# Layer 3 of a four-layer graph network: gathered rows in other places, the table's rows in the last weight matrix

## Chip, core and metric

The kernel runs on one core of one Trainium2 chip. Its time is the device time of one execution in microseconds, and less is better. The profile is one execution on that core, taken by the hardware profiler.

## What is computed

Four layers follow each other on x (2708 nodes x 512 features) with a weighted adjacency matrix adj (2708 x 2708). Each has the form x = x + f(relu(layernorm(x)), adj). Layer 0 is a weighted aggregation, layer 1 an attention, layer 2 two aggregations with dense layers between. The change is in layer 3:

```python
def _L3_gnn_ref(input_features, adj, W, b):
    ...
    A = (adj != 0).astype(input_features.dtype)
    hidden = input_features @ W + b
    deg = jnp.sum(A, axis=0)
    return A @ hidden / deg[:, None]
...
# layer 2: what comes just before
h = jax.nn.relu(adj @ (x @ W1) + b1)
h = jax.nn.relu(adj @ (h @ W3) + b3)
return jnp.tanh(h @ Wf + bf)
```

## The kernel before

**Tiles.** The 2708 nodes make NT = 22 row tiles of 128 (the last, tile 21, has 20 rows). The adjacency is sparse towards the later nodes. So a row tile takes the first DENSE = 6 column tiles whole, and of the other columns only those in which one of its rows has a nonzero. Of these a list was made in layer 0, in chunks of 128 columns: CHUNKS gives 0, 10, 9, 8 chunks for row tiles 0 to 3, seven each for 4 to 7, six for most that follow, and two for tile 21.

**Layer 2** goes through the row tiles in `order_2` (0, then from 6 on, and 1 to 5 last). For each, `aggregated` sums the dense part (right-hand sides ghi, glo and gs of `g_parts`, one set for each of the six dense tiles) and the listed part. For the latter `gather` (L935) lets POOL fetch 128 rows of a table in DRAM for each chunk with an indirect DMA, into one of NGG = 8 tiles gg0 to gg7, in turn. Then come two projections, `project3` (L900): with wf, the last weight matrix but one, whose three parts lie in wa0 to wa2 of the pool wset; after tanh, residual and norm, with w, the last one, whose three parts lie in wb0 to wb2 of wsetb. The result is one row tile of `hid`, the table of layer 3, written to DRAM (L1294), and for tiles from 6 on to `hidr` as well.

**Layer 3** needs A @ hid, with A of zeros and ones. Products are single-pass: `split_h` splits each right-hand side into a rounded high part (ScalarE, L1111) and a remainder (VectorE, L1113), and `add_h` (L1171) makes one matmul of each. There are three kinds of work:

- `whole_h(m)`: the six dense tiles (ghi, glo) with masks a_hi from the stored marks `nz` (L1184).
- `listed_products(m)`: the gathered rows of row tile m. The high part takes one of six tiles of `part_room` (v_hi, v_lo, v_s, two buffers each), the remainder stays where the row was gathered. For the first row tile `behind` (L164) holds the part tiles until dense tile 4 has been split.
- `full_steps()`: row tiles 0 to 3 (FULL) have no usable list and take the whole table, so `load_full` brings rows 768 to 2707 of hid into SBUF: four tiles of 128 rows in each of four buffers (16 loads on SP's queue, L1222). Their high parts go to gs1 to gs5, in turn. The 16 steps are interleaved with the other row tiles, from the third on; the first four take dense tiles alone.

**Places for gathered rows.** `gather_h(m)` takes one place for each chunk from the generator `room()`. Before the change that is: the four quarters of wr (the raw weights' buffer); then again and again eight gg tiles and the four quarters of wb0, wb1 or wb2. Thus row tile 4 has wr (4) and gg (3), row tile 5 gg (5) and wb0 (2), row tile 6 wb0 (2) and gg (5), and row tile 7 gg (3) and wb1 (4). A place can be written only when its former contents have been read.

**Order.** Row tiles 4 to 20 (21 in the middle) are taken in `order_3`. The gathers of the first two are put into the program at the last row tile of layer 2, before its last two projections, the third's right after; from then on gathers are AHEAD = 3 row tiles in front. The program's order gives priorities only: each engine's own order is drawn up by the compiler, which brings an instruction forward when its buffers and inputs are there. Within an engine's queue, the order is then fixed, and POOL's gathers wait in it for their places.

`split_w` and `project3` are those of layer 2; they are unchanged. The functions that the change touches:

Of the kernel before, what the change touches and what calls it, by code (L numbers as in the profile page):

```python
# [9 lines left out]
FP = mybir.dt.float32  # L10
# [12 lines left out]
P = 128  # L23
# [13 lines left out]
DENSE = 6  # L37
# [5 lines left out]
def kernel(  # L43
# [29 lines left out]
    N, D = x.shape  # L73
    H, _, DK = wk_d.shape
# [3 lines left out]
    NCD = D // P  # L78
# [8 lines left out]
    def rows(t):  # L87
        return min(P, N - t * P)
# [63 lines left out]
    def span(t):  # L152
        return slice(t * P, t * P + rows(t))
# [8 lines left out]
    def behind(dst, last):  # L162

        nc.vector.tensor_copy(dst, last)  # L164

    def load_w(pool, src, name, first=None):
        w = pool.tile([P, NCD, D], FP, name=name)
        if first:
            first(w)
        nc.sync.dma_start(out=w, in_=src.rearrange("(c p) k -> p c k", p=P))  # L170
        return w
# [45 lines left out]
    wset = short.enter_context(tc.tile_pool(name="wset", bufs=1))  # L217
# [6 lines left out]
    with tc.tile_pool(name="l0_slab", bufs=2) as slabs, tc.tile_pool(  # L224
        name="l0_h", bufs=1
    ) as hp, tc.tile_pool(name="l0_w", bufs=2) as wp, tc.tile_pool(
        name="l0_acc", bufs=2, space=PSUM
    ) as ps_acc, tc.tile_pool(name="l0_small", bufs=1, space=PSUM) as ps_small, tc.tile_pool(
        name="l0_list", bufs=3, space=PSUM
    ) as ps_list, tc.tile_pool(name="l0_tr", bufs=1, space=PSUM) as ps_tr, tc.tile_pool(  # L230
        name="l0_y", bufs=1, space=PSUM
# [181 lines left out]
        NGG = NT - DENSE  # L413
# [352 lines left out]
        for m in range(NT):  # L766
# [45 lines left out]
            if m == NT // 2 + 6:  # L812
                wr = load_w(wset, w1_d, "wr", lambda w: behind(w[:1, 0, :1], xt[:1, :1]))
                w1 = split_w(wset, wr, "wa")
                wr = load_w(wset, w3_d, "wr")
# [12 lines left out]
    gp = short.enter_context(tc.tile_pool(name="g", bufs=1))  # L828
    wsetb = short.enter_context(tc.tile_pool(name="wsetb", bufs=1))
# [8 lines left out]
    NGG = 8  # L838
# [15 lines left out]
    def gathered():  # L854
        name = f"gg{gather_slot[0] % NGG}"
        gather_slot[0] += 1
        return gp.tile([P, D], FP, name=name)
# [217 lines left out]
    wr = load_w(wset, wf_d, "wr")  # L1075

    for m in order_m:
        n = rows(m)
        parts = aggregated(m, first_parts, first_product, g1d, bias1, marked=True)
        if m == 0:  # L1080
            wf = split_w(wset, wr, "wa")
            wr = load_w(wset, w_d, "wr")
# [43 lines left out]
    def room():  # L1126


        quad = wset.tile([P, NCD, D], FP, name="wr")
        for c in range(NCD):  # L1130
            yield quad[:, c, :]
        i = 0
        while True:
            for _ in range(NGG):
                yield gathered()
            quad = wsetb.tile([P, NCD, D], FP, name=f"wb{i % 3}")
            i += 1
            for c in range(NCD):
                yield quad[:, c, :]

    places_h, part_slot = room(), [0]

    def part_room():
# [73 lines left out]

    def load_full():
        for i, t0 in enumerate(range(DENSE, NT, NCD)):
            quad = wset.tile([P, NCD, D], FP, name=("wa0", "wa1", "wa2", "wr")[i])  # L1220
            for t in range(t0, min(t0 + NCD, NT)):
                nc.sync.dma_start(out=quad[: rows(t), t - t0, :], in_=hid[span(t)])  # L1222
                full_h[t] = quad[:, t - t0, :]
# [89 lines left out]
    for i, m in enumerate(order_3):  # L1313
        listed_products(m)
        if i < AHEAD:
            whole_h(m, DENSE - 1)
        finish_h(m)
        if i == 0:
            load_full()
        if i + AHEAD < len(order_3):  # L1320
            k = order_3[i + AHEAD]
            gather_h(k)
            whole_h(k)
        if i > 1:
            next(steps, None)
        if i == 1:
            some = wp.tile([P, 1], FP, name="some", bufs=1)
            nc.vector.tensor_reduce(some, bad, AX.X, ALU.add)
            tot = ps_t.tile([P, 1], FP, name="pt")
            nc.tensor.matmul(tot, ones, some, start=True, stop=True)  # L1330
            nc.vector.tensor_scalar_min(some, tot, 1.0)
            nc.vector.tensor_copy(flag, some)
# [8 lines left out]
    with tc.If(general > 0):  # L1341

        with tc.tile_pool(name="l0_g", bufs=2) as gp, tc.tile_pool(
            name="l0_gh", bufs=1
# [53 lines left out]
        with tc.tile_pool(name="l1_qkv", bufs=1) as qkvp:  # L1398
# [6 lines left out]
            with tc.tile_pool(name="l1_pw", bufs=1) as pwp, tc.tile_pool(  # L1405
                name="l1_ph", bufs=2
            ) as php, tc.tile_pool(name="l1_px", bufs=3) as pxp, tc.tile_pool(
                name="l1_pps", bufs=2, space=PSUM
# [43 lines left out]
            with tc.tile_pool(name="l1_bias", bufs=2) as bp, tc.tile_pool(  # L1452
                name="l1_p", bufs=2
            ) as pp, tc.tile_pool(name="l1_pT", bufs=3) as ptp, tc.tile_pool(
                name="l1_x", bufs=1
            ) as xp, tc.tile_pool(name="l1_st", bufs=4) as stp, tc.tile_pool(
                name="l1_s", bufs=2, space=PSUM
            ) as ps_s, tc.tile_pool(name="l1_t", bufs=2, space=PSUM) as ps_t, tc.tile_pool(
                name="l1_o", bufs=1, space=PSUM
# [84 lines left out]
        with ExitStack() as gen:  # L1544
# [8 lines left out]
            gp = l2.enter_context(tc.tile_pool(name="g", bufs=2))  # L1553
# [213 lines left out]
```

## Time and profile before

Three runs took 1498.87, 1499.95 and 1506.9 us.

| What | Value |
|---|---|
| median of the runs | 1499.95 us |
| the profiled execution's own time | 1489.76 us |
| its span, first to last instruction | 1488.0 us |
| mean granted TensorE clock | 0.941 |
| TensorE busy | 1298.3 us (87%) |
| VectorE busy | 946.2 us (64%) |
| ScalarE busy | 690.3 us (46%) |
| POOL busy | 657.6 us (44%) |
| moved by DMA | 349.04 MB, mean 235 GB/s |
| the 65 gathers of hidr into gg | 68.5 us busy, 1053 ns each |

Busy time is the time in which an engine worked on at least one instruction, and idle time stands with the event that ended it, its releaser. "Issue" there is idle time for which the profile shows no releaser, "remote" a releaser that it couldn't name. Layer 3 begins at about 1290 us of the span and ends with it. In instruction names, L987 is line 987 of the kernel, and "gg<-hidr,idx_h" an instruction that writes a tile gg and reads hidr and idx_h; numbers of buffers are left out, so wb stands for wb0 to wb2. PE is TensorE, PEld its weight loads, DVE VectorE, ACT ScalarE, SP the queue from which most plain transfers are issued.

### The profile page before, as it was taken

Reading aid. Unit: us, or ns where it says so; the run is one execution under the profiler, and the core shown is the slowest. Engines: PE = TensorE matmul, PEld = TensorE weight load, DVE = VectorE, ACT = ScalarE, POOL = GpSimd, SP = SyncE. Lnnn points to the kernel's source line nnn. Section 1 sums busy time; section 2 is a strip of 40 time slices with the busy share of each in tenths; the row PEclk is TensorE's granted clock in tenths of the full one; section 3 lists DMA queues with packets and bytes.
Section 4 is the critical chain, followed back from the end, with each engine's and each line's share of the span. In section 5 each row is a group of like instructions: output and inputs, shape, how many; then the busy total and the mean of one; then the engine's idle time right before and its main releaser. Section 6 shows DMA issues by size and latency. Waiting matters only on the chain.

```text
span 1488.0 us, 15510 instructions
## 1 busy us (share of the span) xinstructions
PE 1298.3 (87%) x4430; PEld 774.4 (52%) x4430; DVE 946.2 (64%) x1932; ACT 690.3 (46%) x1051; POOL 657.6 (44%) x673
## 2 busy tenths in 40 slices
PE   3987687878958849988999999899999999877997
PEld 1333233333423337745665666466666666555776
DVE  3685776869969769743343446365666656665686
ACT  5965543463256246432333334344445444554453
POOL 1254366565754432054544442244334335326652
PEclk9997789899989979999999999999999999988999
DMA  9977887978797498366777777756555666557885
GB/s 349 375 244 249 268 272 242 315 242 247 250 341 284 145 308 279 131 220 209 252 222 233 237 233 234 243 176 187 174 173 170 195 195 202 175 193 221 275 261 159
DMA packets 200056, 349.04 MB, mean 235 GB/s; under 512 B 26406, under 2 KB 113024, under 8 KB 196229
## 3 DMA queue, kind: packets, MB, share of 16 engines
q1 hardware_dynamic: 149177, 200.80, 40.7%
q0 software_dynamic: 46032, 145.05, 31.2%
q10 hardware_dynamic: 4752, 2.10, 0.6%
q8 instruction: 37, 0.61, 0.2%
q14 instruction: 58, 0.48, 0.1%
HBM read 284.58 MB, written 63.29 MB: 234 GB/s over the span
## 4 chain that ended last, share of the span: by engine, by line
PE 51%; issue 5%; DMA 3%; DVE 2%; another core or an unknown queue 2%; POOL 1%; ACT 1%; SPq 0%; DVEq 0%; ACTq 0%; POOLq 0%
PE aggs L987 14%; PE main L900 9%; PE agg L984 8%; PE mixed L900 4%; PE aggs L984 4%; PE pt L875 3%; PE agg L1171 2%; PE aggs L1171 2%; DMA raw<-in_adj_t_dram 1%; PE aggs L999 1%; PE agg L900 1%; PE pt L1171 1%; POOL wb L935 1%; PE mixed L1171 1%
## 5 line engine op out<-in xcount | busy, mean ns | idle before, releaser
L987 PE MATMUL aggs<-gg,ac 128*128 128x512 f32 (+1 forms) x520 | 232.3, 594 | 3.4 <-DMA gg<-g1d,idx_g 3.4
L935 POOL DMA_INDIRECT gg<-g2d,idx_g x130 | 131.1, 1008 | 220.2 <-PE aggs L987 170.7
L935 POOL DMA_INDIRECT gg<-g1d,idx_g x130 | 133.9, 1030 | 180.1 <-PE aggs L987 109.0
L778 PE MATMUL acc<-h,inc 128*128 128x512 f32 (+1 forms) x348 | 171.1, 632 | 19.6 <-DVE inc L630 14.1
L562 POOL DMA_INDIRECT ac<-in_adj_t_dram,idx_a x130 | 127.9, 984 | 133.4 <-DMA lst<-ac 62.3
L987 PEld LDWEIGHTS aggs<-gg,ac 128*128 128x128 f32 (+1 forms) x520 | 97.9, 189 | 110.6 <-issue 103.0
L580 POOL DMA_INDIRECT h<-h0d,idx_g x111 | 117.2, 1056 | 57.0 <-issue 28.7
L971 ACT ACTIVATE a_hi<-raw 128x384 fp32r<-128x384 f32 x84 | 43.6, 520 | 167.3 <-issue 92.2
L778 PEld LDWEIGHTS acc<-h,inc 128*128 128x128 f32 (+1 forms) x348 | 66.7, 201 | 99.0 <-issue 81.5
L984 PE MATMUL agg<-ghi,a_hi 128*128 128x512 f32 x252 | 114.8, 456 | 3.3 <-ACT a_hi L971 2.4
L158 PE MATMUL yacc<-wvo,hT 128*128 128x512 f32 (+1 forms) x176 | 91.0, 663 | 28.8 <-issue 23.3
L778 PE MATMUL acc<-h,incl 128*128 128x512 f32 (+1 forms) x222 | 102.3, 609 | 0.0
L984 PE MATMUL agg<-glo,a_lo 128*128 128x512 f32 x252 | 102.2, 405 | 0.0
L972 DVE TENSOR_TENSOR a_lo<-raw,a_hi 128x384 fp32r<-128x384 f32 x84 | 47.3, 563 | 85.3 <-ACT a_hi L971 51.0
L984 PE MATMUL aggs<-gs,a_s 128*128 128x512 f32 x252 | 100.3, 401 | 0.6 <-DVE gs L204 0.6
L935 POOL DMA_INDIRECT gg<-hidr,idx_h x65 | 68.5, 1053 | 51.1 <-issue 11.3
L881 DVE SCALAR_TENSOR_TENSOR v_lo<-pt,v_hi 128x512 fp32r<-128x512 f32 (+1 forms) x88 | 56.5, 664 | 41.8 <-ACT v_hi L880 23.4
L862 DVE SCALAR_TENSOR_TENSOR u<-aggs,u 128x512 f32<-128x512 f32 x42 | 28.9, 687 | 77.9 <-PE aggs L987 68.3
L158 PEld LDWEIGHTS yacc<-wvo,hT 128*128 128x128 f32 (+1 forms) x176 | 35.2, 209 | 77.4 <-issue 66.1
L778 PEld LDWEIGHTS acc<-h,incl 128*128 128x128 f32 (+1 forms) x222 | 42.9, 195 | 54.4 <-issue 53.0
L880 ACT ACTIVATE v_hi<-pt 128x512 fp32r<-128x512 f32 (+1 forms) x88 | 48.6, 578 | 45.6 <-PE pt L875 35.8
L542 DVE MAX8 top<-ar 128x8 f32<-128x2708 f32 (+1 forms) x22 | 65.4, 2971 | 0.0
(307 smaller groups left out, 2812.3 us busy)
## 6 DMA issues: line engine op xcount, KB each, us to landing
ar<-in_adj_dram SPq DMA_DIRECT2D x27, 1354.0 KB
raw<-in_adj_t_dram SPq DMA_DIRECT2D x122, 192.0 KB
slot<-x SPq DMA_DIRECT2D x41, 256.0 KB
at<-in_adj_t_dram SPq DMA_DIRECT2D x27, 384.0 KB
ranks<-rank_b SPq DMA_DIRECT2D x20, 485.0 KB
ac<-lst SPq DMA_DIRECT2D x16, 384.0 KB
h<-in_x_dram SPq DMA_DIRECT2D x21, 256.0 KB
h0d<-h POOLq DMA_DIRECT2D x21, 256.0 KB
```

Of the source, the lines that this page charges most:

```text
L158: nc.tensor.matmul(acc[:n], hT[:, c, :n], w[:, c, :], start=(c == 0), stop=(c == NCD - 1))
L542: nc.vector.max(top[:n], ar[:n])
L562: nc.gpsimd.indirect_dma_start(out=ac[:, c, :n], out_offset=None, in_=adj_units, in_offset=bass.IndirectOffsetOnAxis(ap=idx_a[:, m, c0 + c ...
L580: nc.gpsimd.indirect_dma_start(out=g, out_offset=None, in_=h0d[:, :], in_offset=bass.IndirectOffsetOnAxis(ap=idx_g[:, m, c : c + 1], axis=0),)
L778: nc.tensor.matmul(acc[:n], a, g, start=(i == 0), stop=(i == len(pairs) - 1))
L880: nc.scalar.activation(hi[d], pt[d], AF.Relu, scale=UP)
L881: nc.vector.scalar_tensor_tensor(lo[d], pt[d], 0.0, hi[d].bitcast(FP), op0=ALU.max, op1=ALU.subtract)
L900: nc.tensor.matmul(acc[:n], a[:, c, :n], b[:, c, :], start=first and c == 0, stop=last and c == NCD - 1,)
L935: nc.gpsimd.indirect_dma_start(out=gs[c], out_offset=None, in_=gd[:, :], in_offset=bass.IndirectOffsetOnAxis(ap=index[:, m, c : c + 1], ax ...
L984: nc.tensor.matmul(acc[:n], a[:k, i, :n], b[:k], start=st, stop=sp)
L987: nc.tensor.matmul(mixed[:n], a, g, start=(c == 0 and not dense_of(m)), stop=(c == len(chunks) - 1),)
L1171: nc.tensor.matmul(bank_h(m)[: rows(m)], a, b, start=(i == 1), stop=(i == total))
```

## The change

Two functions change. In `room()`, the places from the thirteenth on: after wr and eight gg come gs1 to gs5, once (the third parts of the dense right-hand sides of layer 2), and then again and again the four quarters of wa0, wa1 or wa2 (wf) and eight gg. In `load_full()` the first three buffers of the table's rows are wb0 to wb2 (w) instead of wa0 to wa2; the fourth stays wr. Row tile 5 now has its last two rows in gs1 and gs2, row tile 6 has gs3 to gs5 and wa0, row tile 7 has seven gg, and row tile 8 has gg, the four of wa1, and gg. No instruction is added or removed.

```diff
@@ room()
         quad = wset.tile([P, NCD, D], FP, name="wr")
         for c in range(NCD):
             yield quad[:, c, :]
+        for _ in range(NGG):
+            yield gathered()
+        for t in range(1, DENSE):
+            yield gp.tile([P, D], FP, name=f"gs{t}")
         i = 0
         while True:
-            for _ in range(NGG):
-                yield gathered()
-            quad = wsetb.tile([P, NCD, D], FP, name=f"wb{i % 3}")
+            quad = wset.tile([P, NCD, D], FP, name=f"wa{i % 3}")
             i += 1
             for c in range(NCD):
                 yield quad[:, c, :]
+            for _ in range(NGG):
+                yield gathered()
@@ load_full()
         for i, t0 in enumerate(range(DENSE, NT, NCD)):
-            quad = wset.tile([P, NCD, D], FP, name=("wa0", "wa1", "wa2", "wr")[i])
+            pool, name = ((wsetb, "wb0"), (wsetb, "wb1"), (wsetb, "wb2"), (wset, "wr"))[i]
+            quad = pool.tile([P, NCD, D], FP, name=name)
             for t in range(t0, min(t0 + NCD, NT)):
                 nc.sync.dma_start(out=quad[: rows(t), t - t0, :], in_=hid[span(t)])
                 full_h[t] = quad[:, t - t0, :]
```

## The prediction, made before the changed kernel was run

> **What bounds the kernel now.** I read the page first: TensorE is busy 87% of the span, and the chain that ended last belongs to it for 51%. The change touches layer 3 alone, so next I asked for busy times by stretch from the last rows of layer 2 on. Columns: stretch, its length, then busy us (and instructions) of PE, PEld, DVE, ACT, POOL, granted clock, DMA share, GB/s.
>
> ```profile
> 1290.00:1326.00 36.00, 24.89 (x90) 18.31 (x89) 21.03 (x45) 18.56 (x28) 1.38 (x2) 0.81 0.41 137
> 1326.00:1356.00 30.00, 19.32 (x73) 14.47 (x72) 14.86 (x29) 14.15 (x25) 18.56 (x20) 0.86 0.72 230
> ...
> 1376.00:1400.00 24.00, 22.99 (x100) 18.32 (x100) 15.01 (x29) 11.51 (x20) 16.07 (x17) 1.00 0.86 271
> ...
> 1425.00:1475.00 50.00, 49.18 (x216) 39.50 (x214) 37.63 (x73) 27.20 (x49) 25.08 (x24) 1.00 0.74 224
> ```
>
> From 1376 us TensorE is full (22.99 of 24, clock 1.00). The 66 us before that, where layer 2 hands over to layer 3, are the loose part: 44.2 us busy of 66, clock 0.81 and 0.86, and POOL, which does the gathers, all but empty for the first 36 us. The timeline of POOL says why (start, length, what, and in brackets the idle time before it with its releaser):
>
> ```profile
> 1289.27 1.34 POOL L935 DMA_INDIRECT gg<-hidr,idx_h  x1 [0.30 <-issue]
> 1325.22 0.95 POOL L935 DMA_INDIRECT wb<-hidr,idx_h  x1 [34.62 <-issue]
> ```
>
> Twelve gathers (places 1 to 12: wr and gg) are out by 1290.6. The thirteenth goes to wb, which is the last weight matrix, and that is read by the last row of layer 2 until 1326.5: POOL stands 34.6 us. The timeline of TensorE then shows the holes that follow:
>
> ```profile
> 1315.90 0.79 PE L1171 MATMUL agg<-ghi,a_hi 128*128 128x512 f32 x1 [6.73 <-ACT ghi L1111]
> ...
> 1337.91 0.50 PE L1171 MATMUL aggs<-v_s,ac 128*128 128x512 f32 x1 [1.57 <-issue]
> ...
> 1343.76 0.80 PE L1171 MATMUL aggs<-gg,ac 128*128 128x512 f32 x1 [5.12 <-DVE gg L1113]
> ...
> 1355.09 0.79 PE L1171 MATMUL agg<-wb,ac 128*128 128x512 f32 x1 [3.99 <-DVE wb L1113]
> ```
>
> Three of them (10.7 us) lie in 1326 to 1356. But who ends them is not a gather. The waits of 1200 to 1488 (waiter, releaser, total us, times, longest):
>
> ```profile
> ACT v_lo L1111 <- PE aggs L1171: 16.7, 7, 5.5
> ...
> DVE slot L1211 <- remote: 7.2, 1, 7.2
> ...
> ACT v_hi L1111 <- DMA gg<-hidr,idx_h: 3.2, 4, 1.4
> ```
>
> ScalarE and VectorE, which split each gathered row in two, wait for TensorE to give back the six part tiles (v_hi, v_lo, v_s, two each), and only 3.2 us for gathered data. The 7.2 us of DVE slot (row tile 4's finish, at 1342.31) wait for products whose last matmul the trace ends at 1334.98. For row tile 5 the same step comes 5.7 us after its last matmul (1353.63 against 1347.90), for row tile 6 0.3 us (1359.99 against 1359.66). The first two fall into trains of gathers issued back to back (1325.22 to 1340.32, 1341.73 to 1351.83); before the third POOL stood 4.3 us. My reading: TensorE's releases arrive late while POOL issues gathers without a pause. That is a coincidence in one trace, not proved.
>
> **What the Trainium skill says.** "DMA: Bandwidth & Descriptors", Anatomy of one DMA — SWDGE (gpsimd) path: about 2.0 us fixed for a DMA of this queue. The trace agrees roughly: the gather issued at 1325.22 landed at 1328.16, 2.9 us. The same page, Queues, rings and completion order: a DMA engine takes turns between the queues that have work, so SP's loads and POOL's gathers slow each other; the trace shows gathers landing 6 us after issue at 1335 to 1340, behind four SP loads. "TensorE: Matmul & The Clock Gate", Part 1: after an idle window of some 3.4 us the clock is halved until TensorE is busy again. The trace agrees: half clock in 1313.55 to 1323.79, 1340.86 to 1347.69 and 1354.51 to 1357.93.
>
> **The change, part by part.**
>
> *Gathers 13 to 17 (gs1 to gs5).* Layer 2's last reader of gs is the dense part of row tile 5, whose last matmul is at 1279.88. So they go at 1290.6: five by 1.25 us (0.95 busy + 0.30), done by 1296.9. Nothing waits behind them; cost nothing, DMA is idle then (0.41).
>
> *Gathers of the wa places (18 to 21, then 30 to 33 and 42 to 45).* wa (the last weight matrix but one) has its last matmuls at 1306.2 to 1309.2. As the twelve free wb places were filled in one train (1325.2 to 1340.3, with one gg between), I expect twelve wa gathers at 1307.5 to 1322.5. Thus row tiles 4, 5 and 6 (21 rows) are in place before 1326, where now the rows of tile 6 come until 1349. Row tile 7 becomes all gg (seven places), free as tiles 4 and 5 are used, from about 1331 on.
>
> *What this is worth.* In 1326 to 1339 VectorE needs 21 x 0.6 us = 12.6 us for the splits and no long train of gathers runs beside them, so the three holes should go, and with them the half clock behind two of them: 9 matmuls from 1343.76 and 6 from 1355.09 with 0.43 instead of 0.23 us between starts, 3.0 us. Upper end 10.7 + 3.0 = 13.7 us; lower end nothing, if the part tiles come back as late as now. I take 9: next in line are row tile 7's gathers, issued from 1331.
>
> *The table's rows leave wa (L1222).* Twelve SP loads of 256 KB now run at 1307 to 1320, on idle DMA engines, and five splits (gs<-wa, wa<-wa,gs) stand in the hole. They aren't free there. The row's chain on VectorE:
>
> ```profile
> 1312.63 0.69 DVE L1286 TENSOR_TENSOR gs<-gs,u 128x512 f32<-128x512 f32 x1 [1.25 <-ACT u L1278]
> 1313.66 0.69 DVE L1113 TENSOR_TENSOR wa<-wa,gs 128x512 fp32r<-128x512 f32 x1 [0.33 <-ACT gs L1111]
> 1314.27 0.69 DVE L176 BATCH_NORM_STATS2 stats<-gs 128x6 f32<-128x512 f32 x1
> 1314.87 0.68 DVE L1113 TENSOR_TENSOR wa<-wa,gs 128x512 fp32r<-128x512 f32 x1
> 1315.46 0.18 DVE L178 BATCH_NORM_AGGREGATE mv<-stats 128x2 f32<-128x6 f32 x1
> ```
>
> Without them the statistics start at 1313.3 and end at 1314.2, and the table load and square root follow at once instead of at 1316.5 and 1317.8: 3.4 us earlier, on the path to the last product. Upper end 3.4. Lower end a loss of 3: the transposes (now 1320.48) then fall into the train of wa gathers, whose twelve could hold TensorE's release back as the 7.2 us above show. I take a gain of 1.
>
> *Where they go (wb).* wb is free from about 1324.5 to 1326.5, so SP's twelve loads (3.1 MB) and the four of wr are issued in 12 x 0.42 + 4 x 0.42 = 6.7 us there. At 372 GB/s, the most that the trace shows for such loads (1315 to 1317.5), the twelve take 8.5 us of the DMA engines, beside row tile 7's seven gathers. The table's rows themselves are late for nobody: their first matmul is at about 1380 or later. Price between 0 and 8.5; I take 1.5, since tile 7's rows are needed only after 1339. Queued behind on SP: hid of row tile 5, read only by row tile 21's gather, and the marks (nz) of tile 8, now loaded at 1353.9.
>
> *The five splits* (VectorE 5 x 0.69 = 3.4 us, ScalarE 3.1) move to after 1338, when gs1 to gs5 are free again. From 1376 VectorE is 63% busy and hides them; in the ramp it isn't hidden. Between 0 and 3.4; I take 0.5. The ring of places keeps its period of twelve, eight gg and four others, so from row tile 8 on nothing changes, and matmuls, bytes and gathers stay the same in number.
>
> **Sum.** 9 + 1 - 1.5 - 0.5 = 8 us; I add 2 (between 0 and 2) for the hole before 1315.90, which shrinks if glo no longer queues behind SP's wa loads (issued 1310.69, landed near 1315.2: 4.5 us, against 2.7 for the load issued at 1294.97). So 10 us off the profiled execution: its own time is 1489.76 (span 1488.0 and 1.8 around it), hence about 1480. The median of the runs shown is 1499.95, 10.2 higher (0.7%), for reasons the trace doesn't show; I take the gain from there: 1490.
>
> **Rivals.**
> 1. *Part tiles, not rows (no change).* For it: 16.7 against 3.2 us in the waits. If TensorE's late releases don't come from the trains of gathers, rows that are there earlier wait in SBUF. Gain: 1 to 3 us of the handover less 2 of moved work, about 1499.
> 2. *Slower: contention at 1326 to 1345.* The full 8.5 us on tile 7's rows, 3.4 us of splits and 3 us of late releases in the wa train, and no hole closed: plus 15 at worst; half of it, 1507, is what I give it. It decides once SP's loads hold tile 7's last row beyond some 1347, where TensorE would run out of tiles 4 to 6.
> 3. *All of it.* 13.7 + 3.4 + 2, less 1: 18 us, 1482.
> 4. *It doesn't do what it says:* the order of the instructions on POOL may put the wa gathers behind blocked gg places, so that only five rows come early. Then 3 to 5 us: 1496.
>
> **How the numbers follow.** My forecast (1484 to 1492) 0.44, rival 3 0.20, rivals 1 and 4 together 0.22, rival 2 0.14. A measurement of this kernel can tell about 0.5% (7.5 us) from no change: faster means under 1492.5. That gives 0.65 faster, 0.21 same, 0.14 slower. The range, 1477 to 1504, leaves out about one in ten on either side: past rival 3's value and into rival 2.
>
> **What would show it.** Right: POOL without the 34.6 us, gathers into gs at 1291 and wa at 1307 to 1322; SP's table loads at 1325 or later; the last product of wb before 1323; no TensorE hole over 2 us from 1326 to 1356 and full clock there. Wrong: holes of the same size with ACT v_lo still waiting for PE (rival 1), or ACT v_hi waiting for DMA gg in 1340 to 1355 (rival 2).

## The result, and the profile after

The changed kernel takes 1491.83 us in the median of 19 runs, against 1501.75 us for the kernel before in the runs beside it: ratio 0.9945, 95% interval [0.9923, 0.9966]. Run again on another chip it takes 1476.32 against 1490.29 us, ratio 0.9909 [0.9876, 0.9942]. The ratio leaves out two slow runs of these 19 and is not the quotient of the two medians, which is 0.9934. So it is faster by 0.5 to 0.9%, near the forecast 1490 us. Its profiled execution took 1484.00 us (span 1482.2, clock 0.945), 5.8 us less than the one before. That one is not among the 19 runs, and at 1489.76 us it lies below all of them. The line numbers of what is quoted from L1144 on are 4 or 5 higher than before, and they shift by a few lines in the experiments too.

Some words that recur: a **train** is a row of gathers that POOL issues with no more than the usual 0.30 us between them. A **hole** is idle time of TensorE. A **release** is the **rise** of TensorE's semaphore by which a matmul tells the other engines that it is done. A **burst** is a group of rises that follow each other at once.

Busy times by stretch of the changed kernel, with the same columns and stretches as above:

```profile
1290.00:1326.00 36.00, 20.81 (x76) 14.91 (x75) 16.19 (x29) 12.93 (x20) 11.75 (x12) 0.82 0.39 120
1326.00:1356.00 30.00, 27.18 (x109) 20.33 (x109) 20.90 (x48) 22.32 (x40) 15.69 (x17) 0.93 0.90 308
1376.00:1400.00 24.00, 23.38 (x100) 18.35 (x100) 17.29 (x34) 11.68 (x20) 16.50 (x17) 1.00 0.84 261
```

The second stretch is what was hoped for: TensorE 27.18 us busy instead of 19.32. The first one got worse, 20.81 instead of 24.89 (part of that is a shift: this execution is 3.0 us later when the handover begins). The forecast sum came out about right because it missed a loss and undersized a gain.

The timeline of POOL, with start, length, and the idle time before in brackets. Of each group of gathers the first and the last are shown:

```profile
1280.81 1.28 POOL L935 DMA_INDIRECT gs<-hidr,idx_h  x1 [6.58 <-PE agg L984]
...
1295.25 0.95 POOL L935 DMA_INDIRECT gg<-hidr,idx_h  x1 [0.30 <-issue]
1317.41 1.14 POOL L935 DMA_INDIRECT wa<-hidr,idx_h  x1 [21.21 <-PE main L900]
...
1331.81 0.95 POOL L935 DMA_INDIRECT wa<-hidr,idx_h  x1 [0.30 <-issue]
1339.70 1.23 POOL L935 DMA_INDIRECT gg<-hidr,idx_h  x1 [6.95 <-PE agg L1175]
```

The wait of 34.62 us is gone; one of 21.21 us stands in its place. But the gs gathers don't follow the seven gg ones: the compiler put them first, and the twelve go out from 1280.81 to 1296.20 without a pause. Twelve wa gathers follow as a second train, 10 us later than forecast. The timeline of TensorE shows what lies between:

```profile
1298.80 2.08 PE L900 MATMUL main<-wa,v_hi 128*128 128x512 f32 x4 [4.67 <-ACT go L861]
...
1325.77 0.80 PE L1175 MATMUL agg<-ghi,a_hi 128*128 128x512 f32 x1 [6.78 <-ACT ghi L1111]
...
1357.09 0.50 PE L1175 MATMUL aggs<-ghi,a_hi 128*128 128x512 f32 x1 [3.80 <-issue]
```

The first hole is new. Before, the same product (row tile 4 by wa) began without one at 1290.98. The instruction that it waits for, on ScalarE's timeline:

```profile
1298.15 0.60 ACT L861 ACTIVATE go<-main 128x512 f32<-128x512 f32 x1 [6.59 <-remote]
```

It reads a product whose last matmul ended at about 1292.9 by the trace, and its release by TensorE's semaphore is recorded at 1298.13, 1.9 us after the last gather of the train. The Trainium skill ("Perfetto Trace Analysis", Tensor Engine Instruction (MATMUL, LD_WEIGHTS)) says that a matmul's end in the profile is an estimate, and that the semaphore is raised after it, once PSUM has acknowledged the write. The order agrees with this trace; the distance of 5.2 us is what the trace shows, not the page.

In the waits of 1200 to 1488 (waiter, releaser, total us, times, longest) what answers to the former 16.7 us is:

```profile
ACT v_lo L1111 <- PE aggs L1175: 8.9, 3, 4.4
ACT v_lo L1111 <- PE agg L1175: 8.5, 4, 5.1
```

Before, the second of these stood at 0.6 us. So this wait for TensorE's releases is as long as it was (17.4 and 17.3 us; 1.4 and 5.9 us more have no named releaser). What became shorter is the time in which TensorE stands: its holes of 0.8 us and more after 1326 fell from 17.2 to 6.5 us.

Two stretches sum this up. **Handover**: from the start of row tile 2's wb product to the start of row tile 5's, the last of layer 2. **Rest**: from that product's end to the last instruction. Both are read from one execution each.

| Execution | handover | hole ahead of row tile 4's wa product | rest |
|---|---|---|---|
| before | 52.55 | none | 161.44 |
| before, again (second chip) | 52.30 | none | 162.15 |
| changed | 58.59 | 4.67 | 147.06 |
| changed, again (second chip) | 56.56 | 3.89 | 145.67 |

The change gains 14.4 and 16.5 us in the rest and gives back 6.0 and 4.3 us in the handover. The profiled times differ by less, 5.8 and 4.9 us, since the changed executions begin the handover 3.0 and 8.1 us later. Up to there TensorE's instructions come in the same order in both kernels, and in the later traces of such chips that point lies anywhere from 5.8 us ahead of the first one's to 21.2 us behind it. So single profiled times can't be compared to a few us; the medians of many runs and stretches within a trace can.

### The profile page after: what moved, and what is told of

Its sections match the earlier page's. It is cut to its first block, busy times and chain, and to the rows that moved or that the text cites. A ratio compares the mean times of both kernels' runs of the same rounds, so it can differ in the third digit from the quotient of the medians.

```text
span 1482.2 us, 15513 instructions
## 1 busy us (share of the span) xinstructions
PE 1295.9 (87%) x4430; PEld 770.6 (52%) x4430; DVE 945.8 (64%) x1932; ACT 688.4 (46%) x1051; POOL 661.2 (45%) x673
## 4 chain that ended last, share of the span: by engine, by line
PE 64%; DVE 11%; DMA 8%; issue 7%; another core or an unknown queue 4%; ACT 4%; POOL 1%; SPq 0%; ACTq 0%; DVEq 0%; POOLq 0%
PE aggs L987 14%; PE main L900 9%; PE agg L984 7%; PE acc L778 6%; PE mixed L900 5%; PE aggs L984 4%; PE agg L1175 4%; PE aggs L1175 3%; PE yacc L158 3%; PE pt L875 3%; DVE at_top L544 2%; DMA raw<-in_adj_t_dram 2%; DVE found L383 2%; PE aggs L999 1%
## 5 line engine op out<-in xcount | busy, mean ns | idle before, releaser
L562 POOL DMA_INDIRECT ac<-in_adj_t_dram,idx_a x130 | 131.4, 1011 | 120.5 <-issue 37.3
L935 POOL DMA_INDIRECT gg<-hidr,idx_h x62 | 62.9, 1015 | 49.2 <-issue 16.6
```

Of the source, the lines that this page charges most:

```text
L562: nc.gpsimd.indirect_dma_start(out=ac[:, c, :n], out_offset=None, in_=adj_units, in_offset=bass.IndirectOffsetOnAxis(ap=idx_a[:, m, c0 + c ...
L935: nc.gpsimd.indirect_dma_start(out=gs[c], out_offset=None, in_=gd[:, :], in_offset=bass.IndirectOffsetOnAxis(ap=index[:, m, c : c + 1], ax ...
```

## Experiments

The twelve runs were made on four chips, so each is compared with the kernel before on its own chip. The theories are A (gathers issued without a pause hold back TensorE's releases) and its rivals. The expectations misname some things. What they call row tile 3's wa product is row tile 4's, and "row tile 3's first wb product" is row tile 2's. The "aggregation of row tile 4" is that of row tile 5. The pauses in the kernel before cover row tiles 5 to 9, and "row tile 6 whole" is row tile 5 whole. The handover is the stretch they speak of. Edits are shown against the changed kernel where nothing else is said, and "..." marks what is left out.

### First four: one half of the change at a time, and the train turned round or paused

**e1_swap.** The places go on as before, but with wa, and the table in wb.

```diff
-        for _ in range(NGG):
-            yield gathered()
-        for t in range(1, DENSE):
-            yield gp.tile([P, D], FP, name=f"gs{t}")
         i = 0
         while True:
+            for _ in range(NGG):
+                yield gathered()
...
-            for _ in range(NGG):
-                yield gathered()
```

> The new order of weight matrices alone: rows from the thirteenth on in wa as in the change, the table in wb, but no row in gs. Theory A (a long unbroken train of gathers on GpSimd holds back TensorE's releases; the change's five gs gathers made the train at 1281 twelve long and cost some 6 us ahead of layer 3): with seven gathers in that train TensorE has no hole of 4 us ahead of the wa product of row tile 3, the train of twelve wa gathers is out by about 1325, and the ramp into layer 3 is as good as the change's; time 1484 to 1490, ratio to before 0.988 to 0.992. Theory B (only how early the rows come counts, the hole at 1294 has another cause than the train's length): five rows come later than in the change and the hole stays, so 1493 to 1499, ratio 0.994 to 0.998.

**e2_gs_only.** The five gs places stay. What follows is wb, and the table is in wa, as before.

```diff
-            quad = wset.tile([P, NCD, D], FP, name=f"wa{i % 3}")
+            quad = wsetb.tile([P, NCD, D], FP, name=f"wb{i % 3}")
...
-            pool, name = ((wsetb, "wb0"), (wsetb, "wb1"), (wsetb, "wb2"), (wset, "wr"))[i]
+            pool, name = ((wset, "wa0"), (wset, "wa1"), (wset, "wa2"), (wset, "wr"))[i]
```

> The five rows in gs alone: the rows after them in wb and the table in wa, as before. Theory A: the train at 1281 has twelve gathers, so the hole of 4 to 5 us ahead of the wa product of row tile 3 is there and the handover to layer 3 ends 6 us late; the wb gathers wait for the last wb product as before, with five fewer rows missing; time 1497 to 1504, ratio 0.997 to 1.002. Theory B: five rows early are most of what is wanted, ratio 0.993 to 0.996, as the change.

**e3_gs_last.** The changed kernel, its gs gathers held by VectorE: a copy of one element into each place waits for `last_u[0]`, the tile u of the row tile that layer 2 aggregated last.

```diff
-            yield gp.tile([P, D], FP, name=f"gs{t}")
+            late = gp.tile([P, D], FP, name=f"gs{t}")
+            behind(late[:1, :1].bitcast(FR), last_u[0][:1, :1])
+            yield late
```

> The change, with its five gs gathers put behind the aggregation of row tile 4 by one-element copies on VectorE, so that the seven gg gathers go first and the five gs ones follow them at once: the order is turned round, the train stays twelve long. Theory A: the hole stays, since TensorE's releases of 1290 to 1294 still fall into the train: 1489 to 1494, ratio 0.993 to 0.996, as the change. Rival C (it is the gs gathers going first that does it, by making the gg ones late or by waiting for row tile 4's last part tiles): the hole goes, 1484 to 1488, ratio 0.989 to 0.991.

**e4_gs_pause.** The same, but VectorE holds only the first place, POOL writes it six times over, and copies of one element on POOL hold all five places behind that:

```diff
+            if t == 1:
+                behind(late[:1, :1].bitcast(FR), last_u[0][:1, :1])
+                for _ in range(6):
+                    nc.gpsimd.memset(late, 0.0)
+                hold = gp.tile([1, 1], FP, name="hold")
+                nc.gpsimd.tensor_copy(hold, late[:1, :1])
+            nc.gpsimd.tensor_copy(late[:1, :1].bitcast(FR), hold)
```

> As the kernel with the gs gathers last, and six memsets on GpSimd between the seven gg gathers and the five gs ones, a pause of some 3 us in the train; nothing else is changed. Theory A: the releases go out in the pause, the hole of 4.7 us ahead of row tile 3's wa product is gone or under 2 us, the time 1484 to 1489, ratio 0.988 to 0.992. Theory B or C: as the kernel with gs last, or 0 to 1 us longer: the pause only delays five gathers.

| Run | ratio to before, 95% interval | handover | rest |
|---|---|---|---|
| e1_swap | 0.9968 [0.9951, 0.9985] | 53.7 | 146.3 |
| e2_gs_only | 0.9939 [0.9917, 0.9962] | 52.4 | 142.7 |
| e3_gs_last | 0.9925 [0.9899, 0.9952] | 51.0 | 143.1 |
| e4_gs_pause | 0.9955 [0.9936, 0.9973] | 55.1 | 142.7 |

Theory A fails here. All four ratios lie outside its ranges, e3_gs_last's by a hair. And e2_gs_only has the train of twelve (1216.0 to 1231.8 in its trace) and no hole ahead of row tile 4's wa product. It isn't a slow handover either, 52.4 us. But this chip is another: the kernel before takes 1418.49 us on it. And its semaphore events differ. Some 1360 of the 4430 matmuls raise TensorE's semaphore, and the trace records these rises. In each of these four runs all of them are there, 9 lie more than 0.08 us from the end of a matmul that raises it, and no two are closer than 0.08 us. In the trace of before only 1141 are recorded, 204 of them lie off such an end, and 111 follow another within 0.08 us; in that of the changed kernel 1117, 172 and 109. (Records of the other engines are missing there as well, but those that exist are on time: off are 7 of VectorE's 1279 and 2 of ScalarE's 719.) So on the first chip releases of TensorE come late and in bursts, and on this one they don't. e2_gs_only's POOL issues 61 gathers from 1261.9 to 1344.0 without a pause, and TensorE has no hole over 1.21 us in that time. Among its waits of 1200 to 1406 those for gathered data stand first:

```profile
ACT v_hi L1111 <- DMA gg<-hidr,idx_h: 13.2, 8, 5.7
...
ACT v_lo L1111 <- PE agg L1175: 6.5, 4, 3.2
...
ACT v_lo L1111 <- PE aggs L1175: 4.4, 1, 4.4
```

Over all three part tiles and the whole rest, ScalarE waits 19.7 us for data and 21.4 for TensorE there, against 5.0 and 37.7 in the trace of before (10.3 more have no named releaser). So where releases are on time more of the waiting is for rows, and five early rows bring 0.6% with no help from any train. There the rest is as short with wb (142.7) as with wa (143.1) once the five gs rows are early.

e3_gs_last isn't the test it was meant to be: the copies wait for row tile 5, so the gs gathers start 7.5 us after the last gg one and the train isn't twelve long. In e4_gs_pause the memsets push them further, into the wa gathers: 17 in one train up to 1260.0. The hole that row tile 5's handover has in every version (6.78 us at 1325.77 above) is 8.30 us there, against 6.85 in e3_gs_last.

### Second four: both kernels again, and two mixtures

**e5_after_again** and **e6_before_again** are the two kernels, unaltered.

> The changed kernel once more, unaltered, to compare the experiments with on one chip. Theory A (the gs gathers lengthen a train and cost some 6 us ahead of layer 3): the hole ahead of row tile 3's wa product is again over 4 us and the stretch from row tile 3's first wb product to the last one again some 58 us, ratio 0.993 to 0.996. Rival D (that hole belonged to one execution: the first four runs have it at 0 to 1.6 us whatever the train's length): hole 0 to 1.7 us, that stretch 51 to 54 us, ratio 0.991 to 0.994. The rest, from the last wb product to the end, 143 to 147 us under both.

> The kernel before once more, unaltered, for a trace from this chip. A and D: the stretch from row tile 3's first wb product to the last 51 to 54 us, and from there to the end 150 to 161 us, with four or more TensorE holes of over 1 us in the 90 us after the last wb product, since rows are missing. If the rest is under 147 us with no such holes, the change's gain does not come from rows that come early.

**e7_gs_last_wb** is e2_gs_only with the held gs places of e3_gs_last. **e8_gs_two** is e2_gs_only with two gs places:

```diff
-        for t in range(1, DENSE):
+        for t in range(1, 3):
```

> Five rows in gs behind the aggregation of row tile 4, the rows after them in wb and the table in wa as before: the two halves that did best, together. Rows-early theory: as the kernel with gs alone with its hole of 1.5 us ahead of the wa product gone: ratio 0.991 to 0.994. If wa and wb change nothing once five rows are early, it equals the kernel with gs last (0.9925) within 0.002; if wa's earlier rows are worth something, it is 0.002 to 0.004 above that.

> Two rows in gs in place of five, all else as in the kernel with gs alone, so that the row tile before last of the first three is whole, and the third lacks five of its seven rows until wb is free. Rows-early theory: three of five rows more to wait for at 1.25 us each leaves 3 to 4 us of the gain of 8.6 us unrealised: ratio 0.995 to 0.998. If it isn't the rows but the shift of all later gathers by five places, two fifths of the gain: ratio 0.997 to 0.999. If the gain was of the first two rows (row tile 6 whole) alone: 0.993 to 0.995.

| Run | ratio to before, 95% interval | handover | rest |
|---|---|---|---|
| e5_after_again | 0.9909 [0.9876, 0.9942] | 56.6 | 145.7 |
| e6_before_again | one run, 1489.42 us | 52.3 | 162.2 |
| e7_gs_last_wb | 0.9922 [0.9898, 0.9946] | 50.1 | 150.9 |
| e8_gs_two | 0.9939 [0.9916, 0.9962] | 51.9 | 159.0 |

On this chip (1490.29 us before) releases are late again: in the four traces 69 to 106 rises follow another within 0.08 us. The hole of the changed kernel is back in e5_after_again (TensorE's timeline), so it didn't belong to one execution, and D falls. (The ratio is better than A and D said.)

```profile
1302.49 2.08 PE L900 MATMUL main<-wa,v_hi 128*128 128x512 f32 x4 [3.89 <-ACT go L861]
```

In e7_gs_last_wb, seven gathers and the five later, it is gone, and the handover is 6.5 us shorter than in e5_after_again. It is gone in e8_gs_two as well, where two gs gathers go ahead of the seven with a pause of 0.95 us between. So going first is not what makes the hole. By time alone, though, e7_gs_last_wb can't be told from the changed kernel: their intervals overlap.

e6_before_again has three holes of over 1 us in the 90 us after the last wb product, where I had expected four or more. The rest grows with the rows that must wait for wb: 145.7 us with five gs rows and wa, 150.9 with five gs rows and wb, 159.0 with two, 162.2 with none. e8_gs_two's ratio fits the guess that the first two rows are all of the gain; its stretches don't (handover and rest together 210.9 us against 214.5 in e6_before_again, 202.3 in e5_after_again). Why its runs are that fast stays open.

### Third: pauses in the kernel before, and gs last again

**e9_before_pauses.** The kernel before, with a memset on POOL ahead of each gather of row tiles 5 to 9 (against the kernel before):

```diff
         for c in range(CHUNKS[m]):
+            if index is idx_h and m in (5, 6, 7, 8, 9):
+                nc.gpsimd.memset(gs[c], 0.0)
```

> The kernel before with nothing but a memset of 0.5 us on GpSimd ahead of each gather of the rows of row tiles 6 to 9 (its own buffer, overwritten by the gather): the gathers come 0.5 us apart further, the rows come later, the places stay. Theory A in its present form (while gathers follow each other without pause TensorE's releases get out one per gather, some 1.4 us apart, and go out all together in a pause; on a chip where this doesn't happen, as on the one of the first four runs, it has no effect): on a chip of this kind the TensorE holes of 2 to 5 us in the 40 us after the last wb product shrink although the rows are later: stretch from the last wb product to the end 150 to 158 us in place of 162, ratio 0.990 to 0.997. Theory B (how early the rows come is all that counts): the rows of two tiles come 3 to 7 us later, stretch 163 to 168 us, ratio 1.001 to 1.005. On a chip without late releases both say 1.000 to 1.004.

**e10_gs_last_again** is e3_gs_last, unaltered.

> The change with its five gs gathers behind the aggregation of row tile 4, again, in case this chip releases late as the one of the second four runs did. Theory A: seven gathers, a pause of some 8 us, five gathers: no hole over 1.2 us ahead of row tile 3's wa product (3.9 us with twelve in one train), the stretch from row tile 3's first wb product to the last one 50 to 52 us (56.6 in the changed kernel), the rest as the changed kernel's, 145 to 148 us; ratio 0.985 to 0.989 on such a chip. Theory D (the hole belongs to the chip, not to the train): hole and stretch as in the changed kernel, ratio 0.990 to 0.992. On a chip without late releases 0.991 to 0.994.

This chip (1503.43 us before) releases late as well. e10_gs_last_again: ratio 0.9895 [0.9848, 0.9941], handover 51.2, rest 148.8. POOL's and TensorE's timelines:

```profile
1310.11 1.34 POOL L935 DMA_INDIRECT gg<-hidr,idx_h  x1 [0.30 <-issue]
1318.56 1.40 POOL L935 DMA_INDIRECT gs<-hidr,idx_h  x1 [7.10 <-DVE gs L164]
```

```profile
1312.32 1.19 PE L900 MATMUL main<-wa,v_hi 128*128 128x512 f32 x4 [0.31 <-issue]
```

Seven gathers, a pause of 7.1 us, and the hole is 0.31 us, with the same bytes gathered into the same places. That is what A said of this stretch. The ratio lies between what A and D said and decides nothing.

e9_before_pauses is slower than before, ratio 1.0062 [1.0036, 1.0088], rest 167.9 us. By its time alone theory B wins. Its trace says more. VectorE's finishes of the first row tiles of layer 3 (timeline) in e6_before_again, where the last wb product ends at 1325.48:

```profile
1341.21 0.75 DVE L1211 SCALAR_TENSOR_TENSOR slot<-agg,rdeg,slot 128x512 f32<-128x512 f32 x1 [7.21 <-remote]
1347.16 0.75 DVE L1211 SCALAR_TENSOR_TENSOR gs<-aggs,rdeg,gs 128x512 f32<-128x512 f32 x1 [2.08 <-PE aggs L1171]
1355.71 0.75 DVE L1211 SCALAR_TENSOR_TENSOR slot<-agg,rdeg,slot 128x512 f32<-128x512 f32 x1 [0.39 <-PE aggs L1171]
1368.70 0.75 DVE L1211 SCALAR_TENSOR_TENSOR slot<-aggs,rdeg,slot 128x512 f32<-128x512 f32 x1
```

and in e9_before_pauses, where it ends at 1341.91:

```profile
1350.38 0.75 DVE L1213 SCALAR_TENSOR_TENSOR slot<-agg,rdeg,slot 128x512 f32<-128x512 f32 x1
1355.62 0.74 DVE L1213 SCALAR_TENSOR_TENSOR gs<-aggs,rdeg,gs 128x512 f32<-128x512 f32 x1
1368.16 0.74 DVE L1213 SCALAR_TENSOR_TENSOR slot<-agg,rdeg,slot 128x512 f32<-128x512 f32 x1
1378.13 0.74 DVE L1213 SCALAR_TENSOR_TENSOR slot<-aggs,rdeg,slot 128x512 f32<-128x512 f32 x1
```

Counted from that end the four come 15.7, 21.7, 30.2 and 43.2 us later in the first and 8.5, 13.7, 26.3 and 36.2 us later in the second: 4 to 8 us earlier, with the rows in the same places and gathered at a slower pace. The last memset ends at 1388.12. Then POOL issues 20 gathers in one train, from 1388.29 to 1413.43, and the releases stop coming: between 1392.12 and 1416.84 a single rise is recorded, at 1411.90. On ScalarE's timeline a split that needs a part tile back from TensorE:

```profile
1416.98 0.62 ACT L1113 CAST v_lo<-gg 128x512 fp32r<-128x512 f32 x1 [14.35 <-remote]
```

The last landing event recorded of its row is at 1406.32. What it still waited for came when the train was over, in a burst of 13 rises that begins at 1416.84. POOL stood until the same burst, and TensorE has holes just ahead. POOL's and TensorE's timelines:

```profile
1412.49 0.94 POOL L937 DMA_INDIRECT wb<-hidr,idx_h  x1 [0.30 <-issue]
1417.25 1.06 POOL L937 DMA_INDIRECT gg<-hidr,idx_h  x1 [3.82 <-remote]
```

```profile
1404.86 0.40 PE L1173 MATMUL aggs<-ghi,a_hi 128*128 128x512 f32 x1 [1.01 <-issue]
1406.27 0.58 PE L1173 MATMUL aggs<-glo,a_hi 128*128 128x512 f32 x1 [1.02 <-issue]
...
1412.42 0.79 PE L1173 MATMUL aggs<-ghi,a_hi 128*128 128x512 f32 x1 [2.73 <-issue]
...
1415.40 0.59 PE L1173 MATMUL aggs<-ghi,a_hi 128*128 128x512 f32 x1 [1.75 <-issue]
```

The mask for the matmul at 1412.42 was made by VectorE only from 1411.92 on, after 9.03 us of waiting, so that hole follows from a late release. The matmuls from 1404.86 to 1409.10 are another matter: they read dense tiles and a mask that was there, the profile shows nothing that they wait for, and they go out 1.4 us apart, as the rises within a train do. TensorE itself seems held there; by what, no run shows.

The seventh row tile is finished 20.2 us after the sixth (1420.05 and 1399.86), where e6_before_again needs 10.1. So the pauses let the releases out, and the delay came back, larger, where they stopped. That is a reading of two traces, from two chips.

### Fourth: pauses to the end of layer 3, and the swap again

**e11_gs_last_pauses** is e3_gs_last with a memset ahead of every second gather of row tile 6 and all after it:

```diff
+            if index is idx_h and m > 5 and c % 2:
+                nc.gpsimd.memset(gs[c], 0.0)
```

> The change with its gs gathers last, and a memset of 0.5 us on GpSimd ahead of every second gather of the rows of row tile 6 and all after it, to the end of layer 3, so that no train stays without pause. Theory A: the stretch from the last wb product to the end 142 to 147 us on a chip that releases late (148.8 without the pauses), since no release waits over 3 us; ratio 0.983 to 0.988. Rival E (the gathers come 0.25 us apart further in the mean, rows are late again, as when the kernel before got its pauses): 150 to 156 us, ratio 0.990 to 0.995. On a chip without late releases 0.992 to 0.996 under both.

**e12_swap_again** is e1_swap, unaltered.

> The new order of weight matrices alone, again, in case this chip releases late. Theory A: seven gathers at 1281, so no hole over 1 us ahead of row tile 3's wa product; twelve wa gathers as one train in the handover; the rows from the thirteenth on some 17 us earlier than before, as the stretch from the last wb product to the end shows: 148 to 154 us (162 before, 146 with five rows in gs as well); the time 0.992 to 0.996. If the five gs rows are all of the gain: 158 to 162 us and 0.997 to 1.001. On a chip without late releases as in the first four runs, 0.995 to 0.998.

| Run | ratio to before, 95% interval | handover | rest |
|---|---|---|---|
| e11_gs_last_pauses | 0.9933 [0.991, 0.9957] | 51.3 | 154.0 |
| e12_swap_again | 0.9955 [0.9933, 0.9978] | 51.9 | 152.9 |

On this chip (1500.7 us before, late releases too) the pauses did what they should to the releases: in the last 200 us of e11_gs_last_pauses 24 rises follow another within 0.08 us, against 73 in e10_gs_last_again. The time got no better. The rest is 5 us longer, with a hole of 5.05 us at 1445.4 behind a gathered row that landed at 1448.34: rival E, by the stretch and by the ratio. The two were not run on one chip, but there is no sign that pauses everywhere bring more than they cost in late rows.

e12_swap_again: with seven gathers in the train no hole ahead of row tile 4's wa product, and 9 us off the rest. So on such a chip the swap alone is worth about 9 us there, the five gs rows alone 11 (e7_gs_last_wb) and both 13 to 16 (the changed kernel twice and e10_gs_last_again), each against the 161.4 and 162.2 us of before on other chips.

## Why the prediction came out right, step by step

The number came out right in part by luck: two errors cancelled. Of the signs named for being right, POOL's 34.6 us are gone and the table loads came after 1325. The gathers into gs and wa came at other times, the last wb product ended at 1335.15 instead of before 1323, a hole of 3.80 us ends at 1357.09, and the clock was halved from 1323.44 to 1330.27.

- **The gs gathers "at 1290.6, cost nothing".** This step failed. They went first, at 1280.81, and made a train of twelve, which cost 4.3 to 6.0 us of handover. With the train broken (e10_gs_last_again, e7_gs_last_wb) the loss is gone. I had seen the late releases behind trains in layer 3 and named them a coincidence, and priced them for the train of wa gathers (a loss of 3 at the lower end), but not for this one.
- **The wa gathers "at 1307.5 to 1322.5".** One train of twelve, as forecast, but at 1317.41 to 1332.8. The row tile that reads wa last came 9.8 us later than before: 3.0 us were there when the handover began, the rest is that hole and the half clock behind it (the product took 4.93 us instead of 2.95). The train that I took as a pattern held eleven wb gathers and one gg, not twelve and one. e12_swap_again has no such hole, and has them from 1308.7 (its first wr gather, 1248.51, is 1.8 us earlier).
- **The ramp, "I take 9".** Undersized: the rest shrank by 14.4 and 16.5 us, beyond the upper end of 13.7, and that net of the table's loads below. The holes of 0.8 us and more account for 10.7 us of the first, the remainder is half clock and shorter ones. Rows that are there bring a gain by themselves (e2_gs_only on the chip without late releases). That releases in time do so too is what the first four row tiles of e9_before_pauses suggest. Which share is which on the first chip stays open.
- **The chain to the last wb product, "a gain of 1".** From row tile 4's wb product to row tile 5's it took 19.76 us before and 19.01 after: 0.75. The upper end of 3.4 wasn't reached, since ScalarE's order has a split of a dense tile ahead of the square root.
- **The table's loads "beside row tile 7's gathers, 1.5".** Undersized. The loads run from 1334.70 to 1346.9. The marks nz of a later row tile, which I had named as queued behind them and priced at nothing, are issued at 1348.78 and land 7.5 us later. On SP's and VectorE's timelines:

```profile
1348.78 0.32 SPq L1160 DMA_DIRECT2D nz<-nz  x1
```

```profile
1356.68 0.63 DVE L1188 CAST a_hi<-nz 128x384 fp32r<-128x384 uint8 x2 [4.93 <-DMA nz<-nz]
```

  That is the hole of 3.80 us at 1357.09, with eight matmuls at half clock behind it, 0.43 instead of 0.23 us apart: 1.6 us more. All the runs with five gs rows and the table in wb have a hole in that place, of 2.9 to 4.4 us (e3_gs_last 3.16, e10_gs_last_again 2.91, e11_gs_last_pauses 4.39). Against the 1.5 it cost some 5 us. What of it is the table's loads and what the gathers beside them wasn't separated.
- **The five splits, "0.5"**: nothing shows them as a wait. **"Plus 2" for the hole before 1315.90**: nothing; it is 6.78 us against 6.73, since the load that it waits for (3.92 us of ScalarE's wait) now lands beside wa gathers.
- **The sum.** Forecast 10 us. Measured 5.8 in the first profiled execution, 9.9 and 14.0 in the medians. By the two stretches: the rest brought 14.4 and 16.5 us where the sum had 9 - 1.5 - 0.5 = 7, and the handover lost 6.0 and 4.3 us where the sum had a gain of 1 + 2. Two errors of 7 to 9.5 us cancelled.
- **The rivals.** Rival 4 is refuted: the wa gathers stood ahead of the blocked gg ones. Rival 1 (part tiles, not rows) was half right: the wait for TensorE's releases is real on such chips and hardly shorter after the change, but TensorE's holes are shorter. Of rival 2 the late releases came true, in another place than it said; of rival 3 the gain of the ramp.

Holding the gs gathers back is the best version measured: 0.9895 [0.9848, 0.9941] and, on the chip without late releases, 0.9925 [0.9899, 0.9952]. Its handover is 5 to 7 us shorter than the changed kernel's, its rest (148.8 us) 2 to 3 us longer. The two were not timed on one chip, and the intervals overlap, so that it beats the change is likely and not shown.

## What to carry to other kernels

When buffers come free for early loads, look at where the compiler puts these loads in their queue, not only at whether the queue is idle: five gathers "into an idle stretch" lengthened a train at the most delicate place of the kernel. A stall whose named releaser ended long before is a price to be carried to every other place with the same cause. And run the control on the same chip: an effect of 5 us here was absent on one of the chips. A single line of the waits can mislead as well: here 16.7 us shrank to 8.9, and the neighbouring line grew by as much.

## What the runs showed of the hardware

- On every chip but that of the first four runs TensorE's semaphore rises come late while POOL issues gathers back to back, one per 1.25 us. In the traces of both kernels, of both again and of e9_before_pauses there are 25 bursts of five or more rises after 900 us. All begin while POOL issues nothing, 22 of them 1.0 to 1.9 us after the end of a train's last gather, and POOL's next gather, which mostly waits for just these rises, starts 0.3 to 2.6 us later. In 24 of the 25 packets of the last gather still move when the burst begins, so it isn't the end of the transfers that lets the rises out. Beside a train they come one at a time, as at 1341.18, 1342.60, 1344.01 and 1345.41 in e6_before_again, 1.40 us apart, where three gathers go out from 1341.40 to 1345.25.
- In a burst they are 0.034 us apart (eleven from 1365.58 to 1365.92 in e6_before_again). The Trainium skill ("TensorE: Matmul & The Clock Gate", The cost: per-tile semaphore tail) says of the matmuls of a tiled array that their increments serialize, at 26.3 ns each in its fit. The spacing here, of other matmuls, is of that size; what holds the rises back until then no run here shows.
- On the chip of the first four runs all rises are on time beside trains of up to 61 gathers, and the kernel before (1418.49 us against 1490 to 1503) and its variants take some 5% less. In the four traces 42 to 47 us of the lead over the trace of before are there after the first 300 us, ahead of anything that the change touches. That late releases are the cause of it wasn't tried.
